# A graph layer's double product in 49 small products instead of 28 large ones, with streams of their own

## The chip, the cores and the metric

The kernel runs on one core of a Trainium2 chip. The metric is the device time of one execution in microseconds (us). The engines that matter here: TensorE (PE, matrix products into the eight banks of PSUM), VectorE (DVE), ScalarE (ACT) and GpSimd (POOL) for elementwise work, and SyncE (SP), which issues all DMA transfers of this kernel from one queue, in order. Each engine works through its own instructions in program order and waits on semaphores of the others.

## The reference

There are 64 graphs of N = 256 nodes with D = 512 features, all in f32. Layer 0 is a three-layer graph convolution with a residual and a layer norm; layer 1 is a graph attention with a residual and a layer norm.

```python
# layer 0
h = relu(adj @ (x @ W1) + b1)
h = relu(adj @ (h @ W2) + b2)
x1 = layernorm(x + adj @ (h @ W3) + b3)
# layer 1
q, k = split(x1 @ Wqk);  v = x1 @ Wv
agg = adj @ (k * mask)
w = mask * sum(q * agg, axis=-1) / sqrt(512)
out = layernorm(x1 + softmax(w, over nodes) * v)
```

The kernel uses M = Wq Wk^T: sum(q * (adj (x1 mask) Wk)) is sum((x1 M) * (adj (x1 mask))). So it needs x1 @ Wv and x1 @ M, the *double product*: x1 times two weights side by side, 512 by 1024 together. Scores come from the M half and the gathered rows gt = adj (x1 mask); values come from the Wv half.

## The kernel before

Graphs go in 32 pairs (G = 2). `front` (line 347) does for pair i: support with W1, aggregate with adj, support W2, aggregate, support W3. `back` (line 376) does for pair i-1: the third product with adj plus residual, layer norm, transposition of x1, the gather gt, and then `attention(0)` and `attention(1)`, the double product of each graph, one after the other. `finish` (line 501) does for pair i-2: softmax, values, second layer norm and output. These three are Python generators; each `yield` ends a step, and `run` (line 537) takes steps in the order of a string with a letter per step: ORDER (line 532) with F, B and E for the 31 steady periods, START for the first pair and END for the last. There is no other scheduler: each engine's instructions stand in the order in which the steps record them.

Every large product uses `seven` (line 102), the seven-product form of a 2x2 block product. With sums of the blocks on both sides, products 1, 7, 6, 2, 5, 3, 4 go into three banks: x collects 1, 6, 5, 3; v collects 7 and 4; y holds 2. In between, ACT copies x to temporaries (t1 after product 1, u after 6, q after 5), and PE's next product into x has to wait for that copy. DVE adds t1, q, u to y and v for the blocks of the result; with `plus`, POOL adds a residual to the temporaries first.

- `support` (line 247): 28 matmuls of 128x256 columns per call. The sums of its left side are POOL's (`a_sums`, line 225: S0 = lower blocks' sum, S1, S2, S3). 
- `aggregate` (line 266): 16 matmuls of 128x256, with relu and bias by ACT.
- `adj_times` (line 301): 14 matmuls of 128x256; its sums are POOL's too (`adj_sums`, `t_sums`).
- `attention(g)` (line 445): for each graph, seven products of two matmuls each of 128x512 columns (two for the halves of the inner dimension). Its weights `mv` are Wv, M and their four differences, kept in SBUF for the whole run; its left side is x1T and four sums of x1T made by POOL.

x1 is transposed by DVE in 32x32 blocks, written to `via` in DRAM and read back by four DMAs (lines 430 to 436), so x1T lies with a stride: elements of one block are 16 elements apart. SP issues per pair: xT of the next pair, via, four x1T reads, out twice, aT, x.

What the steps of the change touch: `seven` (102), `load_w` (140), `make_m` (196), `a_sums` (225), `adj_sums` (286), `t_sums` (296), `front` (347), `back` (376), `finish` (501), the orders (532) and the main loop (548).

Of the kernel before, what the change touches and what calls it, by code (L numbers as in the profile page):

```python
# [20 lines left out]
def gcn_then_graph_attention(ctx: ExitStack, tc: tile.TileContext, xT, xN, adjT, mask, W1, b1, W2, b2, W3, b3,  # L21
                             WqT, WkT, Wv, out):

# [66 lines left out]
    def b_sums(B, Ts, eng):  # L90

        sub = OP.subtract
        eng.tensor_tensor(Ts[2], B[3], B[1], op=sub)  # L93
        eng.tensor_tensor(Ts[0], B[1], B[0], op=sub)
        eng.tensor_tensor(Ts[1], B[3], Ts[0], op=sub)
        eng.tensor_tensor(Ts[3], B[2], Ts[1], op=sub)

    def shaped(shape):
        t = tmp()
        return t.rearrange("p (a b) -> p a b", a=shape[1]) if len(shape) == 3 else t  # L100

    def seven(mm, shape, c11, c12, c21, c22, plus=None):

        x = bank(shape)
        mm(1, x, True)
        t1 = shaped(shape)
        nc.scalar.copy(t1, x)  # L109
        if plus is not None:  # L110
            padd(t1, t1, plus[0])
        yield
        v = bank(shape)
        mm(7, v, True)
        yield
        mm(6, x, False)
        u = shaped(shape)
        nc.scalar.copy(u, x)  # L118
        yield
        y = bank(shape)  # L120
        mm(2, y, True)
        c11(y, t1)
        yield
        mm(5, x, False)
        q = shaped(shape)
        nc.scalar.copy(q, x)  # L126
        if plus is not None:
            padd(q, q, plus[2])
            padd(u, u, plus[1])
        c22(v, q)  # L130
        yield
        mm(3, x, False)
        c12(x)
        yield
        mm(4, v, False)
        c21(v, u)
        yield


    def load_w(w, n):  # L140
# [14 lines left out]
        def end():  # L155
            load(2)
            b_sums(q, ts, nc.vector)
            return {1: q[0], 2: q[2], 3: q[3], 4: ts[3], 5: ts[0], 6: ts[1], 7: ts[2]}
# [11 lines left out]
    warm(10)  # L170
    begin, end = load_w(W1, 1)
    xTs = load_xT(0, begin)
    wl = [end()]
# [6 lines left out]
    for n, w in ((2, W2), (3, W3)):  # L180
        begin, end = load_w(w, n)
        begin()
        wl.append(end())
    aTs[1] = load_adj(1)
    b3b = const.tile([P, D], FP, name="b3b")
    nc.sync.dma_start(b3b, b3.partition_broadcast(P))
    mask_t = const.tile([P, NH, NPAIR * G], FP, name="mask_t")
    nc.sync.dma_start(mask_t, mask.rearrange("p (h b) -> p h b", h=NH))
    mask_s = const.tile([P, NH, NPAIR * G], FP, name="mask_s")
    nc.vector.tensor_scalar(mask_s, mask_t, ISCALE, None, op0=OP.mult)  # L190
# [3 lines left out]
    mv = {}  # L194

    def make_m():

        wq = pool.tile([P, DC, D], FP, name="wqT", tag="r", bufs=1)
        qk = [[wq[:, d] for d in range(DC)],
              [pool.tile([P, D], FP, name="wkT", tag="T", bufs=4) for _ in range(DC)]]  # L200
        for d in range(DC):
            for t, w in ((qk[0][d], WqT), (qk[1][d], WkT)):
                nc.sync.dma_start(t, w[d * P:(d + 1) * P, :])
        m = [pool.tile([P, 2, D], FP, name="m0", tag="v", bufs=2), const.tile([P, 2, D], FP, name="m1")]
        v0 = const.tile([P, 2, D], FP, name="v0")
        nc.sync.dma_start(v0, Wv[:HD].rearrange("(c p) f -> p c f", p=P))
        v1 = const.tile([P, 2, D], FP, name="v1")
        nc.sync.dma_start(v1, Wv[HD:].rearrange("(c p) f -> p c f", p=P))
        yield
        for f in range(DC):  # L210
            pt = bank((P, D))
            for d in range(DC):
                for j in range(DC):
                    nc.tensor.matmul(pt[:, j * P:(j + 1) * P], lhsT=qk[0][d][:, f * P:(f + 1) * P],  # L214
                                     rhs=qk[1][d][:, j * P:(j + 1) * P], start=(d == 0 and j == 0),
                                     stop=(d == DC - 1), skip_group_check=True)
            nc.scalar.copy(m[f // 2][:, f % 2, :], pt)
            yield
        ts = [const.tile([P, 2, D], FP, name=f"mv_{s}") for s in KEYS]
        b_sums((v0, m[0], v1, m[1]), ts, nc.vector)  # L220
        mv.update({1: v0, 2: v1, 3: m[1], 4: ts[3], 5: ts[0], 6: ts[1], 7: ts[2]})
        yield


    def a_sums(blk, eng=nc.gpsimd):
# [3 lines left out]
        S = [pool.tile([P, 2, G, P], FP, name="S", tag="S", bufs=11) for _ in range(4)]  # L229
# [17 lines left out]
    def support(src, w, last=None):  # L247
# [3 lines left out]
        def mm(n, ps, first):  # L251
            for g in range(G):
                for c in range(2):
                    nc.tensor.matmul(ps[:, g], lhsT=src[n][:, c, g], rhs=w[n][:, c], start=(first and g == 0 and c == 0),  # L254
                                     stop=(g == G - 1 and c == 1), skip_group_check=True)
# [10 lines left out]
    def aggregate(C, aT, b):  # L266


        hT = [pool.tile([P, 2, G, N], FP, name="hT", tag="act", bufs=4) for _ in range(2)]
# [16 lines left out]
    def adj_sums(aT):  # L286
# [3 lines left out]
        padd(S[:, 0], blk(1, 0), blk(1, 1))  # L290
        padd(S[:, 1], S[:, 0], blk(0, 0), sub)
        padd(S[:, 2], blk(0, 0), blk(1, 0), sub)
        padd(S[:, 3], blk(0, 1), S[:, 1], sub)
        return {1: blk(0, 0), 2: blk(0, 1), 4: blk(1, 1), 5: S[:, 0], 6: S[:, 1], 7: S[:, 2], 3: S[:, 3]}

    def t_sums(B):
        Ts = [pool.tile([P, G, HD], FP, name="T", tag="T", bufs=4) for _ in range(4)]
# [49 lines left out]
    def front(i, hT, src, aT):  # L347
        C = yield from support(src, wl[0])
        nxt = load_xT(i + 1) if i + 1 < NPAIR else None
        src, last = yield from aggregate(C, aT, bcol[0])  # L350
        C = yield from support(src, wl[1], last)
        src, last = yield from aggregate(C, aT, bcol[1])
        x = load_x(i)
        steps = support(src, wl[2], last)
        next(steps)
        yield
        next(steps)
        yield
        aS = adj_sums(aT)
        next(steps)  # L360
        yield
        for g in range(G):
            next(steps)
            for h in range(NH):
                padd(x[:, g, h, :], x[:, g, h, :], b3b)
            yield
        nS = None
        if nxt is not None:
            nS, first, rest, last = a_sums(lower_first(nxt))
            first()  # L370
            rest()
            last()
        C = yield from steps
        return C, aS, x, nxt, nS

    def back(i, C, aS, x, end):
# [34 lines left out]
        if end:  # L411
# [3 lines left out]
            for h, g in hg:  # L415
                apply(h, g)
            Ts = t_sums(xmb)
            for h, g in hg:
                pt = bank((P, 2, 2, P))
# [3 lines left out]
        else:  # L423
# [3 lines left out]
            for h, g in hg:  # L427
                apply(h, g)
                for k in range(2):
                    nc.vector.transpose(tr[:, :, :, h, k, :, g].rearrange("p q j c -> p c q j"),  # L430
                                        r[:, g, h, k * HD:(k + 1) * HD].rearrange("p (c q j) -> p c q j", c=2, q=4))
            via = dram.tile([4, P, D], FP, name="via")
# [8 lines left out]
        gb = lambda h, j: gt[:, h, :, j * HD:(j + 1) * HD]  # L441
        w = small.tile([P, NH, G], FP, name="w", bufs=2)
        vs = [None] * G

        def attention(g):
            b = i * G + g
            v = pool.tile([P, NH, D], FP, name="v", tag="v", bufs=2)

            def mm(n, ps, first):
                for c in range(2):  # L450
                    nc.tensor.matmul(ps, lhsT=src[n][:, c, g], rhs=mv[n][:, c], start=(first and c == 0),  # L451
                                     stop=(c == 1), skip_group_check=True)

            def score(y, h):
                nc.vector.scalar_tensor_tensor(y, y, mask_s[:, h, b:b + 1], gt[:, h, g, :], op0=OP.mult,
                                               op1=OP.mult, accum_out=w[:, h, g:g + 1])

            def c22(ps, t):
                add(t, ps, t)
                score(t, 1)  # L460
            vs[g] = v
            yield from seven(mm, (P, D), lambda y, t: add(v[:, 0, :], y, t), lambda x: score(x, 0),
                             lambda ps, t: add(v[:, 1, :], ps, t), c22)
        gather = adj_times(aS, xmb, Ts, lambda y, t: add(gb(0, 0), y, t), lambda x: nc.scalar.copy(gb(0, 1), x),
                           lambda v, t: add(gb(1, 0), v, t), lambda v, t: add(gb(1, 1), v, t))
        src, first, rest, last = a_sums(x1b, nc.vector if end else nc.gpsimd)
        if end:
            first()
            rest()
            last()  # L470
            one = attention(0)
            for k in "GMGMGMGMGGGMMM":
                next(gather if k == "G" else one)
                yield
            for _ in gather:
                pass
            for _ in one:
                pass
            tail = finish(i, (r, vs, w), [0])
            for _ in attention(1):  # L480
                next(tail, None)
                yield
            for _ in tail:
                pass
            for _ in finish(i, (r, vs, w), [1]):
                pass
            return
        for _ in range(4):
            next(gather)
            yield  # L490
        first()
        rest()
        last()
        yield from gather
        if i + 2 < NPAIR:
            aTs[i + 2] = load_adj(i + 2)
        for g in range(G):
            yield from attention(g)
        return r, vs, w

    def finish(i, prev, gs=range(G)):

        r, vs, w = prev
# [4 lines left out]
        for k, g in enumerate(gs):  # L508
            for h in range(NH):
                nc.vector.scalar_tensor_tensor(vs[g][:, h, :], vs[g][:, h, :], s[:, h, k:k + 1], r[:, g, h, :],  # L510
# [4 lines left out]
        for k, g in enumerate(gs):  # L515
            for h in range(NH):
                nc.vector.bn_stats(st[:, h, k], vs[g][:, h, :])  # L517
# [6 lines left out]
        for k, g in enumerate(gs):  # L524
            for h in range(NH):
                nc.scalar.activation(vs[g][:, h, :], vs[g][:, h, :], AF.Identity, scale=rs[:, h, k:k + 1],  # L526
# [79 lines left out]
```

## Time and profile before

| | us |
|---|---|
| median of three runs | 2838.85 (2838.0 to 2839.55) |
| the profiled execution | 2837.91 |
| its span, first to last instruction | 2836.1 |
| PE busy | 2810.0 |
| POOL busy | 1437.5 |
| DVE busy | 1120.9 |
| ACT busy | 945.3 |

The span is what the profile covers, and the execution's own time has 1.8 us more around it. A matmul of 128x256 or 128x512 in f32 shows as two records. The records of matmuls overlap, since one begins while the one before drains: the duration of a record (380 ns for 256 columns, 592 for 512) is longer than the distance from start to start. "PE busy" is the union of the records. Lines are those of the kernel before. The mean granted TensorE clock is 0.998.

Groups of the page that the change takes away or changes: L451, the double product, 896 matmuls in all: with x1T as weights 384, with its sums 512; L62 `v<-ps,tmp` and `tmp<-ps,tmp`, the adds from PSUM, 692 ns each; L455, the scores, 881 ns from SBUF and 758 ns from PSUM; L233 to L240 `S<-x1T` on POOL, 2190, 1993, 1524 and 1520 ns, against 1270 for such a sum of tiles that lie dense; L109, L118, L126, ACT's copies of x, about 585 ns each.

### The profile page before, as it was taken

The numbers are of one execution on the slowest core, as the hardware profiler recorded it, in microseconds if no ns is written. First come the engines' busy times: TensorE is split into PE (matmuls) and PEld (weight loads), VectorE is DVE, ScalarE is ACT, GpSimd is POOL, SyncE is SP. The second block draws the span as 40 slices with busy tenths as digits, with TensorE's granted clock in tenths as the row PEclk, the third lists the DMA queues.
The fourth block names the chain that finished last, engine by engine and source line by source line (L and its number), as shares of the span: only waits on it lengthen the run. The fifth ranks groups of instructions, "written<-read, shape, count | busy, mean of one in ns | idle before, by whom it ended". The sixth has DMA issues, their size and how long they took to land.

```text
span 2836.1 us, 29920 instructions
## 1 busy us (share of the span) xinstructions
PE 2810.0 (99%) x11344; PEld 2191.4 (77%) x11344; DVE 1120.9 (40%) x2326; ACT 945.3 (33%) x1517; POOL 1437.5 (51%) x1122
## 2 busy tenths in 40 slices
PE   9999999999999999999999999999999999999997
PEld 8887778877778877787777788777887777877774
DVE  2444334443344443344433444333444334443335
ACT  2333233332333332333323333323333233333333
POOL 4545455445555455554555554556545455445551
PEclk9999999999999999999999999999999999999999
DMA  4211222211222112222122221122221222211210
GB/s 153 67 60 42 65 80 82 82 42 55 67 82 82 54 44 67 82 82 73 44 63 67 82 82 45 53 67 82 82 64 49 67 67 82 82 45 52 67 60 30
DMA packets 63086, 191.00 MB, mean 67 GB/s; under 512 B 5728, under 2 KB 8928, under 8 KB 54880
## 3 DMA queue, kind: packets, MB, share of 16 engines
q1 hardware_dynamic: 62944, 189.10, 21.1%
q8 instruction: 90, 1.47, 0.2%
q14 instruction: 52, 0.43, 0.1%
HBM read 123.02 MB, written 66.06 MB: 67 GB/s over the span
## 4 chain that ended last, share of the span: by engine, by line
PE 97%; DVE 1%; DMA 1%; ACT 1%; issue 0%; SPq 0%; POOL 0%; ACTq 0%; DVEq 0%; POOLq 0%
PE ps L254 41%; PE ps L451 27%; PE ps L275 16%; PE ps L307 13%; PE ps L214 1%; DMA aT<-in_adjT 0%; PE ps L341 0%; PE ps L326 0%; DMA mask_t<-in_mask 0%; ACT v L526 0%; SPq L149 0%; DVE st L517 0%; POOL tmp L65 0%; DMA out<-v 0%; DVE st L388 0%
## 5 line engine op out<-in xcount | busy, mean ns | idle before, releaser
L254 PE MATMUL ps<-w_T,S 128*128 128x256 f32 x2304 | 546.9, 380 | 2.3 <-POOL S L237 1.5
L254 PEld LDWEIGHTS ps<-w_T,S 128*128 128x128 f32 x2304 | 432.5, 190 | 106.6 <-issue 52.1
L275 PE MATMUL ps<-aT,sup 128*128 128x256 f32 x2048 | 472.7, 379 | 0.0
L275 PEld LDWEIGHTS ps<-aT,sup 128*128 128x128 f32 x2048 | 389.1, 190 | 76.1 <-issue 22.2
L62 DVE TENSOR_TENSOR sup<-ps,tmp 128x512 f32<-128x512 f32 x288 | 198.4, 689 | 526.8 <-PE ps L254 338.4
L451 PE MATMUL ps<-mv_T,S 128*128 128x512 f32 x768 | 361.0, 592 | 0.0
L65 POOL TENSOR_TENSOR tmp<-tmp,x 128x512 f32<-128x512 f32 x96 | 120.5, 1270 | 418.8 <-ACT tmp L126 242.3
L278 ACT ACTIVATE hT<-ps,b 128x512 f32<-128x512 f32 x256 | 175.4, 685 | 377.1 <-PE ps L275 377.1
L62 DVE TENSOR_TENSOR v<-ps,tmp 128x512 f32<-128x512 f32 x128 | 88.5, 692 | 535.5 <-PE ps L451 531.8
L118 ACT COPY tmp<-ps 128x512 f32<-128x512 f32 x224 | 131.3, 586 | 486.3 <-PE ps L254 223.4
L109 ACT COPY tmp<-ps 128x512 f32<-128x512 f32 x224 | 130.7, 583 | 418.0 <-PE ps L254 283.7
L126 ACT COPY tmp<-ps 128x512 f32<-128x512 f32 x224 | 130.7, 583 | 339.0 <-PE ps L254 221.4
L254 PE MATMUL ps<-w,hT 128*128 128x256 f32 x1024 | 241.9, 379 | 0.0
L451 PE MATMUL ps<-v,x1T 128*128 128x512 f32 x512 | 240.6, 592 | 0.0
L254 PEld LDWEIGHTS ps<-w,hT 128*128 128x128 f32 x1024 | 194.5, 190 | 46.3 <-issue 14.8
L451 PEld LDWEIGHTS ps<-mv_T,S 128*128 128x128 f32 x768 | 145.8, 190 | 102.1 <-issue 92.3
L233 POOL TENSOR_TENSOR S<-x1T 128x512 f32<-128x512 f32 x31 | 67.9, 2190 | 275.7 <-DMA x1T<-via 275.7
L307 PE MATMUL ps<-T,aS 128*128 128x256 f32 x768 | 200.3, 383 | 0.3 <-ACT tmp L109 0.3
L451 PEld LDWEIGHTS ps<-v,x1T 128*128 128x128 f32 x512 | 146.2, 290 | 69.3 <-issue 17.7
L233 POOL TENSOR_TENSOR S<-hT 128x512 f32<-128x512 f32 x64 | 81.2, 1269 | 220.5 <-ACT hT L278 220.5
L254 PE MATMUL ps<-w,S 128*128 128x256 f32 x768 | 181.5, 379 | 0.7 <-issue 0.7
L93 POOL TENSOR_TENSOR T<-sup 128x512 f32<-128x512 f32 x32 | 41.0, 1281 | 272.8 <-ACT sup L256 272.8
(109 smaller groups left out, 4179.9 us busy)
## 6 DMA issues: line engine op xcount, KB each, us to landing
x<-in_xN SPq DMA_DIRECT2D x32, 1024.0 KB, 5.7
out<-v SPq DMA_DIRECT2D x64, 512.0 KB, 3.3
xT<-in_xT SPq DMA_DIRECT2D x31, 1024.0 KB, 4.9
via<-tr SPq DMA_DIRECT2D x31, 1024.0 KB, 4.3
x1T<-via SPq DMA_DIRECT2D x124, 256.0 KB, 4.7
aT<-in_adjT SPq DMA_DIRECT2D x32, 512.0 KB, 4.3
w<-in_W SPq DMA_DIRECT2D x9, 256.0 KB, 5.2
xT<-in_xT SPq DMA_DIRECT2D x2, 512.0 KB, 5.1
```

The source lines that it names most:

```text
L62: nc.vector.tensor_tensor(o, a, b, op=OP.add)
L65: nc.gpsimd.tensor_tensor(o, a, b, op=op)
L93: eng.tensor_tensor(Ts[2], B[3], B[1], op=sub)
L109: nc.scalar.copy(t1, x)
L118: nc.scalar.copy(u, x)
L126: nc.scalar.copy(q, x)
L233: eng.tensor_tensor(S[2], blk(0, 0), blk(1, 0), op=sub)
L254: nc.tensor.matmul(ps[:, g], lhsT=src[n][:, c, g], rhs=w[n][:, c], start=(first and g == 0 and c == 0), stop=(g == G - 1 and c == 1), skip ...
L275: nc.tensor.matmul(ps[:, g], lhsT=C[k][c // 2][:, g, (c % 2) * P:(c % 2 + 1) * P], rhs=aT[:, k, g], start=(g == 0 and k == 0), stop=(g == ...
L278: nc.scalar.activation(hT[c // 2][:, c % 2], ps, AF.Relu, bias=b[:, c:c + 1])
L307: nc.tensor.matmul(ps[:, g], lhsT=aS[n][:, g], rhs=mov[n][:, g], start=(first and g == 0), stop=(g == G - 1), skip_group_check=True)
L451: nc.tensor.matmul(ps, lhsT=src[n][:, c, g], rhs=mv[n][:, c], start=(first and c == 0), stop=(c == 1), skip_group_check=True)
```

## The change

The double product uses the seven-product form twice. The outer form takes the pair's two graphs together: x1 in 2x2 blocks (rows by inner dimension) times [Wv; M] in blocks (inner dimension by the two weights' halves as before), seven outer products. Each outer product is itself done by seven inner products on 128x128 left blocks and 128x256 right blocks. That makes 49 matmuls of 128x256 per pair in place of 28 of 128x512.

Outer products run in four chains: a = (1, 2), b = (6, 5), c = (7, 4), d = (3). A chain of two puts both outer products in one bank (256 columns each), so that one step has two matmuls and one eviction serves both; d has half of that. Chains a and b alternate step by step, then c and d. The sums on the outer right side are taken so that product 5 has the opposite sign: the outer sum P1 + P6 + P5 is then a difference, and the result blocks are P1+P2, C22 = (P1+P6+P5) + P7, C12 = (P1+P6+P5) + P3 and C21 = C22 + P4 - P5. Chains c and d get the outer sums as the `plus` of `seven`.

- Left side: `attention` copies three blocks of x1T on ACT and makes four sums on DVE (Z), and eight sums on POOL (I) for the inner form.
- Right side: 49 blocks of 128x256 are made once at the start (`make_m`) and stay in DRAM (`w_dram`), not in SBUF. A ring of seven tiles feeds PE: each step's matmuls are followed by the issue of the fetch for seven steps later, 28 fetches per pair on SP's queue (21 of 256 KB and 7 of 128 KB).
- Scores now come from SBUF: `results(g)` after the inner products, once for each graph.
- Streams: the sums on POOL for the next pair (`sums`, letter S), the gather (G) and the double product (M) are generators of their own beside F, B and E; the last pair has two finishing streams X and Y. START, ORDER and END are new strings.
- `seven` with `plus` issues c22 and the addition to u after product 3 instead of after product 5.
- W2 and W3 are loaded and summed inside START (`prepare`), not ahead of it.
- Buffers: hT 4 to 2, S 11 to 8, v two of one graph to one of two graphs; the results R lie in the places of T, x1T and Z.

```diff
@@ seven
         nc.scalar.copy(q, x)
         if plus is not None:
             padd(q, q, plus[2])
+        else:
+            c22(v, q)
+        yield
+        mm(3, x, False)
+        if plus is not None:
+            c22(v, q)
             padd(u, u, plus[1])
-        c22(v, q)
-        yield
-        mm(3, x, False)
         c12(x)
@@ 
+    def prepare():
+        for n, w in ((2, W2), (3, W3)):
+            begin, end = load_w(w, n)
+            begin()
+            yield from end()
...
+        yield from make_m()
+    OUTER = ((1, 2), (6, 5), (7, 4), (3,))
+    INNER = (1, 7, 6, 2, 5, 3, 4)
+    STEPS = "ab" * 7 + "cd" * 7
+    w_dram = [dram.tile([P, 7, len(q), HD], FP, name=f"mv_{k}", bufs=1) for k, q in enumerate(OUTER)]
...
+    RING = 7
+    def fetch(k):
+        if k < NPAIR * len(uses):
+            q, n = uses[k % len(uses)]
+            t = pool.tile([P, 2, HD], FP, name="ring", bufs=RING)
+            nc.sync.dma_start(t[:, :len(OUTER[q])], w_dram[q][:, n])
+            ring[k] = t
@@ make_m
+        for q, outer in enumerate(OUTER):
+            for k, n in enumerate(outer):
+                w = pool.tile([P, 7, HD], FP, name="w7", tag=("Za", "Ia")[place[n] % 2], bufs=1)
+                blk = [B[n][:, c, j * HD:(j + 1) * HD] for c in range(2) for j in range(2)]
+                for i, b in ((1, blk[0]), (2, blk[2]), (3, blk[3])):
+                    nc.scalar.copy(w[:, at[i]], b)
+                yield from b_steps(blk, [w[:, at[i]] for i in (5, 6, 7, 4)], nc.vector)
+                nc.sync.dma_start(w_dram[q][:, :, k], w)
+                yield
@@ back: the old attention(g), a_sums(x1b) and the end's own loop go; the gather becomes a stream
-            def mm(n, ps, first):
-                for c in range(2):
-                    nc.tensor.matmul(ps, lhsT=src[n][:, c, g], rhs=mv[n][:, c], start=(first and c == 0),
-                                     stop=(c == 1), skip_group_check=True)
...
-            yield from seven(mm, (P, D), lambda y, t: add(v[:, 0, :], y, t), lambda x: score(x, 0),
-                             lambda ps, t: add(v[:, 1, :], ps, t), c22)
...
-        for g in range(G):
-            yield from attention(g)
+        put["G"] = gather()
+        put["M"] = attention(i, x1b, w, r, put)
+    def attention(i, x1b, w, r, put):
...
+        for n, b in ((1, x1b(0, 0)), (2, x1b(0, 1)), (4, x1b(1, 1))):
+            nc.scalar.copy(z(n), b)
+        for o, a, b, op in ((z(5), x1b(1, 0), x1b(1, 1), OP.add), (z(6), z(5), z(1), sub), (z(7), z(1), x1b(1, 0), sub),
+                            (z(3), z(2), z(6), sub)):
+            nc.vector.tensor_tensor(o, a, b, op=op)
+        yield
+        for s in range(2):
+            padd(I[s][:, 2], Z[s][:, :, 0], Z[s][:, :, 1], sub)
+            padd(I[s][:, 0], Z[s][:, :, 1], Z[s][:, :, 3])
+            padd(I[s][:, 1], I[s][:, 0], Z[s][:, :, 0], sub)
+            padd(I[s][:, 3], Z[s][:, :, 2], I[s][:, 1], sub)
+            yield
...
+            def mm(n, ps, first):
+                wt = ring.pop(at[0])
+                for k, o in enumerate(outer):
+                    nc.tensor.matmul(ps[:, k], lhsT=left[n](place[o]), rhs=wt[:, k], start=(first and k == 0),
+                                     stop=(k == len(outer) - 1), skip_group_check=True)
+                fetch(at[0] + RING)
+                at[0] += 1
...
+        for n, k in enumerate(STEPS):
+            if n == 14:
+                add(B[:, 0], B[:, 0], A[:, 0])
+                yield
+                nc.vector.tensor_tensor(B[:, 0], B[:, 0], B[:, 1], op=sub)
+                yield
+                add(v[:, :, 0], flat(A[:, 0]), flat(A[:, 1]))
+                yield
+                C = pool.tile([P, 2, G, 2, HD], FP, name="R", tag="Za", bufs=1)
+                run.update(c=inner(2, C, B), d=inner(3, B[:, :1], B[:, :1]))
+            if n == 26:
+                yield from results(0)
+            next(run[k])
+            yield
+        yield from results(1)
@@ orders
-    ORDER = ("F E F" + " B F" + " B F E" * 2 + " B B E F E F" + " B F E" + " B F B F F B B F F" +
-             " B F B F B F E B B E F F" + " B F E B F E" + " B F E B F E B B F B F B F B" + " B F B F B B F B F B F B")
+    ORDER = ("BFFFEFFEBEFBBBFBFBBFBFEFBFBFBEBBBGFEGSFFEGGFEGEEFEMFMFFFGMMGSMEMMMMMMMMMMMSMMMMMMFSM"
+             "FMMFSMMMMFFSMMMSEMMSMFMFSMSMSMM")
```

## The prediction

> **What bounds the kernel now.** I read the page's busy line and its 40 slices first, then the chain that ended last, then the waits of PE alone, then PE in order of time inside one period.
>
> ```profile
> span 2836.1 us, 29920 instructions
> ...
> PE 2810.0 (99%) x11344; PEld 2191.4 (77%) x11344; DVE 1120.9 (40%) x2326; ACT 945.3 (33%) x1517; POOL 1437.5 (51%) x1122
> ...
> q1 hardware_dynamic: 62944, 189.10, 21.1%
> ...
> PE 97%; DVE 1%; DMA 1%; ACT 1%; issue 0%; SPq 0%; POOL 0%; ACTq 0%; DVEq 0%; POOLq 0%
> ```
>
> PE is busy for the whole span and is 97% of the chain; the other engines and DMA are half idle. Overlapped records can hide a PE that is not at its peak, so I check its pace:
>
> ```profile
> 910.80 1.88 PE L451 MATMUL ps<-mv_T,S 128*128 128x512 f32 x4
> 912.52 1.88 PE L451 MATMUL ps<-v,x1T 128*128 128x512 f32 x4
> 914.23 1.03 PE L254 MATMUL ps<-w,hT 128*128 128x256 f32 x4
> ...
> 1050.88 5.34 PE L275 MATMUL ps<-aT,sup 128*128 128x256 f32 x24
> 1056.06 1.89 PE L254 MATMUL ps<-w,hT 128*128 128x256 f32 x8
> ```
>
> From start to start, 8 records of 512 columns take 914.23-910.80 = 3.43 us, 0.429 each; 24 records of 256 columns take 5.18 us, 0.216 each. An f32 matmul is two records, so 0.858 and 0.432 us. SP's issues of the next xT mark the period, 86.9 us:
>
> ```profile
> 960.75 0.33 SPq L72 DMA_DIRECT2D xT<-in_xT  x1
> ...
> 1047.66 0.33 SPq L72 DMA_DIRECT2D xT<-in_xT  x1
> ```
>
> Its matmuls: 84 (three supports) + 32 (two aggregates) + 28 (two adjacency products) = 144 of 256 columns, 62.2 us; 28 of 512, 24.0 us; small transposes of the softmax 0.7. Sum 86.9: PE has no hole in a steady period. What is taken from PE's work comes off one for one, as long as nothing else becomes late.
>
> **1. PE work.** 28 matmuls of 512 columns (24.02 us) become 49 of 256 (49 x 0.432 = 21.15): -2.87 us per pair. Weight loads go from 56 to 98 records per pair, but a 190 ns load lies under a 216 ns matmul already in the rows of L254 and L275, and the 290 ns loads of the strided x1T go. 31 of the 32 double products lie in steady periods: **-89.0 us**. The last is in part 5.
>
> **2. The other engines, per period of 84 us.** DVE has 35.0 now (1120.9/32). It loses 10 operations of the old scores and adds (7.9) and gains 14 adds from PSUM at 0.69 or less (8.5), 4 sums into Z, 3 combinations of 1024, 4 scores, 2 adds. The last 13 have both operands in SBUF. Rows for such operations: 0.69 alone, 1.31 and 1.76 beside POOL (lines 233, 236 at the end); for 1024 elements 1.22 and 2.17. So DVE comes to 47 to 55 us. ACT: 29.5, less 6 copies of 0.585, plus 17, three of them from strided x1T: 35 to 37. POOL: 44.9, less the four strided sums (7.2), plus eight I sums (1.27 or about 1.0) and six additions (1.27 or 0.73): 53. All under 84, so none becomes the bound by its total.
>
> The Trainium skill, SBUF — State Buffer, § Who interferes with whom, speaks against this change: VectorE with two SBUF inputs and a GpSimd instruction that reads SBUF exclude each other for the whole instruction. The rows above agree in direction; by the rule 13 DVE operations could each wait one whole POOL sum of 1.27 us, an estimate of 16 us more on DVE, 64 to 72 of 84, and the sum below stays.
>
> **3. Who waits for whom on the way.** I followed the order of the built program from one support 1 to the next, with PE at 0.432 per matmul and the rows' durations for the rest.
> - *x1T to Z.* The trace has 11.3 us from the issue of via to the first sum on x1T. via can be issued 16.3 us after xT, as now, so Z starts 44 us into the period. ACT's three copies end at 46 to 47.5 (0.585 to 1.17 each; strided ACT reads have no row, POOL's strided sum takes 1.7 times the plain one), and the first inner product is due at 48.8. The hT evictions queue behind these copies on ACT, due about 4 us later. Cover 1.3 to 2.8 us; costs nothing.
> - *I sums.* The first is due on PE at 51.4 and ends at 47.5 (49 at worst); the third at 53.1 against 50 to 51.5.
> - *One copy between two accumulations.* Products 5 and 3 of one chain have a single 0.864 us step between them. This line shows what it needs:
>
> ```profile
> 17.30 0.59 ACT L126 COPY tmp<-ps 128x512 f32<-128x512 f32 x1 [2.87 <-PE ps L254]
> ```
>
>   PE's slot before it ended at 15.37 + 8 x 0.216 = 17.10 and PE went on at 17.98: 0.88 us. Loss 0.02 per pair, nothing.
> - *Softmax.* Its two transposes now stand 3.68 us apart (6.9 before). The end of the trace shows the chain: 3.31 us from 2810.74 to 2814.05, table load included. Cover 0.4.
> - *The residual product of B*: c22 and the addition to u now stand behind product 3. c22 has to be done before product 4 writes the same bank, with 1.73 us of F between; the statistics then end at 22.3 and hT_2, which waits behind them on ACT, at 23.3, asked at 25.1. Nothing.
> - *Shared buffers* (v single, hT two, S eight, R in the places of T, x1T and Z): the closest are v, written at 65 when its last out has landed at 57, and T, written at 81 when R's last reader ends at 69.5 (combinations at 2.17). Nothing.
> - *POOL's b3b additions, adjacency sums, S and T sums* end at least 2 us before PE or DVE asks; behind the wait for x stands S_3, asked 6 us later.
>
> **4. The ring of weights.** 28 fetches per pair are new on SP (21 of 256 KB, 7 of 128 KB), each issued when a step's matmul ends, at 0.33 to 0.47 us of SP. SP is in order: aT and the second out<-v stand between them, and that out waits for ACT's last activation, done 9 us before. Seven tiles are there at the start; then step k+7 needs a fetch that was issued 6.05 us before. A lone 256 KB read lands in 3.0 to 3.3 us (the first of the four x1T reads). In sixteen steps of 0.864 the queue must also carry aT and out, four units of 256 KB. With the first fetch on the wire at 52.3, the tenth tile arrives at 52.3 + 7 units + 0.1, due at 57.5. What is a unit?
>
> ```profile
> 0.00:23.00 23.00, 17.66 (x79) 14.66 (x80) 11.77 (x17) 3.63 (x5) 6.42 (x10) 1.00 0.96 327
> ```
>
> In the loading stretch (clock 1.00, then DMA share 0.96, 327 GB/s) full engines would move 341 GB/s: 0.77 us, a tile 0.3 us late. By the page's whole-run share (189.1 MB in 21.1% of 2836.1: 316 GB/s) 0.83 us, 0.75 late. A single slice of the window 900:987 reached 383 GB/s: 0.68, not late. I take the saturated stretch, the nearest: 0.3 us in each of 31 periods, **+9** (0 to +23).
>
> The Trainium skill, DMA: Bandwidth & Descriptors, § Bandwidth, advises batches of 1 MiB or more, and its § Anatomy of one DMA — SWDGE (gpsimd) path (another queue than SP's) gives 2.0 us plus bytes over 436 GB/s, an estimate of 2.6 us for 256 KB. One fetch at a time, that would stop every step; seven deep, it is shorter than 6.05 and costs 0. The measured 3.0 to 3.3 leads.
>
> **5. Start and end.** *Start:* DVE no longer holds support 1's evictions behind the sums of W2 and W3 (PE waits 0.72 and 0.77 at 17.98 and 20.71); one of these goes, about 1.7 us with what follows. The M product moves forward to where its last weights land (issued 19.38, 5.5 us): no gain, up to 4 lost. **-1.5** (-3 to +4). *End:* after the last F matmul (2765.1) the trace runs 71.0 us, two old products (3.4) among them. After: E's four bn_stats (0.68) and three activations (0.8) stand ahead of B's chain on DVE and ACT, so the last double product starts 28.7 us after F instead of 23.1; it is 3 us shorter; but PE stops for about 4.3 us ahead of its last two steps until DVE has the scores of g=0, and behind the last step there are two more adds, two scores and an add, about 5 us. I get 76 us. With the two steps that no longer lie behind F (-3.4+0.4) the end costs 76-71+3 = **+8** (+3 to +13).
>
> **Sum.** -89 + 9 - 1.5 + 8 = -73.5. The profiled execution took 2837.9 (span 2836.1), 0.9 below the median of 2838.85: 2764.4 against it, 2765 for a median. Ends: 2838.85-89+0-3+3 = 2750 and 2838.85-89+23+4+13 = 2790.
>
> **The rivals.**
> - *Slower: the ring's DMA sets the pace.* If a 256 KB unit takes s, the fourteenth tile arrives at 52.3 + 11s + 0.1, due at 60.9: 11s - 8.5 late per pair. The 81 us of parts 1 and 5 are gone at 2.6 us per pair, s = 1.01. For it: 2 KB packets in a 14 KB stride are not in this trace, and the seven-deep ring has only 0.4 us of cover at s = 0.70. Against it: every saturated stretch shows 0.68 to 0.83. At s = 1.2 the time is 2838.85-81+31 x 4.7 = 2904.
> - *DVE and POOL block each other longer than summed up.* Then Z, I and the scores come late in each period: two sums at 1.76 instead of 0.69 eat the cover, and 0.8 to 1.6 us per pair are lost: 2783 to 2807. For it: the rows of 1.76 and 2.17. Against it: POOL is idle while Z is made.
> - *The change doesn't bring what it counts*, since PE waits on several small things (copies behind L617, x late): 1.5 to 2.6 us per pair, 2805 to 2838. Against it: covers of 1 to 6 us.
> - *No stall at all and a cheap end:* 2750 or a little under.
>
> **How the numbers follow.** Forecast with its range 2750 to 2790: 0.62. A cleaner run, under 2750: 0.04. DVE and POOL, up to 2807: 0.11. Several small waits: 0.07, of which 0.02 within 0.2% of 2838.85 (about what a measurement of this kernel can tell from no change). Ring slower than break-even: 0.16, nearly all slower. Range 2748 to 2815 holds about 0.77 and leaves the slower rival out. Faster 0.82, same 0.02, slower 0.16.
>
> **What the profile after would show.** Period between xT loads 84.0 to 84.6 (part 1 and 4); PE's waits: <-DMA ring under 0.5 us per pair if part 4 holds, above 2.6 if the slower rival does; waits <-ACT Z, <-POOL I or <-DVE w in steady periods near 0 (part 3), else the second rival; POOL busy about 1700 us, DVE 1500 to 1760, ACT 1130 to 1180 (part 2); behind the last F matmul 76 us with a PE hole of some 4 us before the last two ring steps (part 5). I would be wrong most if 2 KB reads at a 14 KB stride are slow, or if x1T lands over 2 us later than now.

## The result and the profile after

The changed kernel takes 2833.94 us (median of four runs, 2828.76 to 2836.84), beside 2838.47 for the kernel before on the same chip: a ratio of 0.9981 with a 95% interval of 0.9964 to 0.9999. That is 0.19% faster, less than the 0.2% that the prediction took for no change, and 69 us above the 2765 that was forecast. The profiled execution took 2833.77. (Of the four executions of e5 below, the profiled one ran at a third of TensorE's pace, 8150 us; e5's time is that of the other three, and the trace of that kernel is e9's.)

The page after, busy time, ring queue and the chain that ended last:

```profile
span 2832.0 us, 36770 instructions
...
PE 2740.0 (97%) x12688; PEld 2371.6 (84%) x12688; DVE 1703.6 (60%) x2898; ACT 1151.9 (41%) x1888; POOL 1786.5 (63%) x1446
...
q1 hardware_dynamic: 197568, 401.10, 44.5%
...
PE 86%; DMA 7%; ACT 3%; DVE 3%; issue 1%; POOL 0%; SPq 0%; ACTq 0%; DVEq 0%; POOLq 0%
PE ps L306 37%; PE ps L543 18%; PE ps L328 15%; PE ps L364 14%; DMA ring<-mv 6%; DVE e L391 1%; ACT L388 1%; ACT e L388 1%; ACT tmp L126 1%; ACT tmp L117 1%; PE ps L248 1%; PE ps L398 0%; DVE gt L560 0%; DMA xT<-in_xT 0%; DVE w L97 0%
```

PE fell from 97% of the chain to 86%. What came in its place has names: ring<-mv, the fetches of the double product's weights, and the softmax's e on DVE and ACT. The waits of PE alone, as us in total, number of times, longest, say the same:

```profile
PE ps L543 <- DMA ring<-mv: 33.8, 39, 2.3
PE ps L398 <- DVE e L391: 22.6, 28, 3.6
PE ps L383 <- DVE gt L560: 9.4, 3, 4.0
PE ps L476 <- DVE r L460: 2.9, 2, 1.7
PE ps L306 <- DVE sup L65: 2.1, 1, 2.1
PE ps L306 <- POOL S L289: 1.8, 2, 1.5
```

The two upper rows recur in nearly every pair; the others belong to the start and the end. Before, no wait recurred; the longest row there was this one:

```profile
PE ps L341 <- DVE e L334: 3.7, 2, 2.5
```

This view misses part of a wait that stands inside a group. Counted from start to start of PE's records, at the first record of each step and beyond 0.216 us, the ring loses 45.3 us over 32 pairs: 35.2 at the tenth tile of a pair (in 29 of the pairs, 1.21 us each), 10.1 at the ninth (in 27 pairs, 0.37 each), nothing at the other 26 tiles.

Between SP's issues of xT, averaged over the last 29 periods, a period takes 86.34 us, against 86.90 before and 84.0 in the forecast. So 2.3 us of the 2.87 that the matmuls saved per pair are lost again to waits: about 1.4 to the ring, 0.7 to the softmax, the rest to pieces of 0.08 to 0.1 us.

How one pair loses at the ring: PE and then SP, in order of time (start, duration, line, what; in brackets the idle time and its end).

```profile
1339.35 3.62 PE L543 MATMUL ps<-ring,I 128*128 128x256 f32 x16
1342.80 1.89 PE L543 MATMUL ps<-ring,Z 128*128 128x256 f32 x8
1344.80 1.10 PE L543 MATMUL ps<-ring,I 128*128 128x256 f32 x4
1346.81 2.91 PE L543 MATMUL ps<-ring,I 128*128 128x256 f32 x12 [0.91 <-DMA ring<-mv]
```

```profile
1337.81 0.34 SPq L230 DMA_DIRECT2D ring<-mv  x1
1338.71 0.33 SPq L84 DMA_DIRECT2D aT<-in_adjT  x1
1339.54 0.32 SPq L230 DMA_DIRECT2D ring<-mv  x1
1339.95 0.38 SPq L620 DMA_DIRECT2D out<-v  x1
1340.43 4.61 SPq L230 DMA_DIRECT2D ring<-mv  x6
```

The issues are on time, one fetch whenever PE frees a tile. Between the eighth tile's fetch (1337.81) and the tenth's (1340.43) stand aT and the second out, 512 KB each. In the trace the eighth tile landed at 1340.51, aT at 1344.00, the ninth at 1344.66, out at 1346.33, the tenth at 1346.67; PE goes on at 1346.81. From then on tiles land 0.68 us apart and PE never waits for them. What the 16 DMA engines did meanwhile, in 40 slices of 0.75 us from 1335 on (busy share in tenths, then GB/s):

```profile
DMA  0000089986799999999885968689998585048789
GB/s 0 0 0 0 0 139 330 284 216 123 254 393 399 404 402 388 407 355 243 287 264 182 310 128 303 164 212 412 426 415 358 169 280 176 0 71 306 183 276 341
```

From 1338.75 to 1343.25 they are busy for 60% of the time or more and yet move only 123 to 330 GB/s, 224 in the mean; then, 90% busy or more, 388 to 407.

How the softmax loses, from its first transposes (L383) to its second (L398); `T<-sup,T` are GpSimd's sums for B's product, and `tmp<-tmp,x` adds the residual x to the first copy of that product:

```profile
1378.47 0.38 PE L383 MATMUL ps<-ident,w 128*2 128x128 f32 x2
1378.48 2.94 POOL L97 TENSOR_TENSOR T<-sup,T 128x512 f32<-128x512 f32 x2
1378.89 0.41 DVE L385 TENSOR_REDUCE nmax<-ps 2x1 f32<-2x256 f32 x1
1379.28 1.28 ACT L388 ACT_TABLE_LOAD   x1
1380.58 0.47 ACT L388 ACTIVATE e<-ps,nmax 2x256 f32<-2x256 f32 x1
1381.16 0.15 DVE L390 RECIPROCAL rtot<-tot 2x1 f32<-2x1 f32 x1 [1.86 <-ACT e L388]
1381.35 1.43 DVE L391 TENSOR_SCALAR e<-e,rtot 2x256 f32<-2x256 f32 x1
1381.37 1.27 POOL L68 TENSOR_TENSOR tmp<-tmp,x 128x512 f32<-128x512 f32 x1
1382.93 0.25 PE L398 MATMUL ps<-ident,e 2*128 2x2 f32 x2 [0.62 <-DVE e L391]
```

The scaling of e, 2x256 elements, took 0.341 us in every period before (least, median and greatest duration in ns, then first and last start). Here it takes 1.43 in most, starts with POOL's tmp+x and ends 0.14 us behind it. First the kernel before, then the changed one:

```profile
L334 DVE TENSOR_SCALAR e<-e,rtot x33: 340/341/342, 166.0 to 2826.4; 2x256 f32<-2x256 f32 x31, 1x256 f32<-1x256 f32 x2
L391 DVE TENSOR_SCALAR e<-e,rtot x33: 341/1435/1461, 171.8 to 2821.2; 2x256 f32<-2x256 f32 x31, 1x256 f32<-1x256 f32 x2
```

### The profile page after: what moved, and what is told of

The parts are those of the page before. It is cut to its first block, busy times and chain, and to the rows that moved or that the text cites. A ratio compares the mean times of both kernels' runs of the same rounds, so it can differ in the third digit from the quotient of the medians.

```text
span 2832.0 us, 36770 instructions
## 1 busy us (share of the span) xinstructions
PE 2740.0 (97%) x12688; PEld 2371.6 (84%) x12688; DVE 1703.6 (60%) x2898; ACT 1151.9 (41%) x1888; POOL 1786.5 (63%) x1446
## 4 chain that ended last, share of the span: by engine, by line
PE 86%; DMA 7%; ACT 3%; DVE 3%; issue 1%; POOL 0%; SPq 0%; ACTq 0%; DVEq 0%; POOLq 0%
PE ps L306 37%; PE ps L543 18%; PE ps L328 15%; PE ps L364 14%; DMA ring<-mv 6%; DVE e L391 1%; ACT L388 1%; ACT e L388 1%; ACT tmp L126 1%; ACT tmp L117 1%; PE ps L248 1%; PE ps L398 0%; DVE gt L560 0%; DMA xT<-in_xT 0%; DVE w L97 0%
## 5 line engine op out<-in xcount | busy, mean ns | idle before, releaser
L65 DVE TENSOR_TENSOR R<-ps,tmp 128x512 f32<-128x512 f32 (+1 forms) x384 | 235.4, 620 | 455.1 <-PE ps L543 350.2
L543 PE MATMUL ps<-ring,I 128*128 128x256 f32 x1792 | 435.3, 383 | 36.5 <-DMA ring<-mv 33.8
L328 PE MATMUL ps<-aT,sup 128*128 128x256 f32 x2048 | 457.7, 379 | 0.0
L543 PEld LDWEIGHTS ps<-ring,I 128*128 128x128 f32 x1792 | 332.8, 190 | 107.0 <-ACT tmp L134 40.3
L134 ACT COPY tmp<-ps 128x512 f32<-128x512 f32 (+1 forms) x288 | 158.3, 561 | 473.6 <-PE ps L306 251.3
L68 POOL TENSOR_TENSOR I<-Z 128x384 f32<-128x384 f32 (+1 forms) x128 | 173.3, 1374 | 262.6 <-ACT Z L521 244.9
L543 PE MATMUL ps<-ring,Z 128*128 128x256 f32 x1344 | 327.7, 380 | 0.0
L68 POOL TENSOR_TENSOR tmp<-tmp,R 128x512 f32<-128x512 f32 x192 | 214.9, 1140 | 169.8 <-DVE R L580 141.5
L126 ACT COPY tmp<-ps 128x512 f32<-128x512 f32 (+1 forms) x288 | 158.1, 560 | 358.9 <-PE ps L543 173.8
L117 ACT COPY tmp<-ps 128x512 f32<-128x512 f32 (+1 forms) x288 | 158.7, 563 | 326.7 <-PE ps L364 120.2
L543 PEld LDWEIGHTS ps<-ring,Z 128*128 128x128 f32 x1344 | 256.4, 191 | 34.7
L68 POOL TENSOR_TENSOR x<-x,b3b 128x512 f32<-128x512 f32 x128 | 176.8, 1382 | 73.2 <-DMA x<-in_xN 63.8
```

The costliest lines, as they stand in the source:

```text
L65: nc.vector.tensor_tensor(o, a, b, op=OP.add)
L68: nc.gpsimd.tensor_tensor(o, a, b, op=op)
L328: nc.tensor.matmul(ps[:, g], lhsT=C[k][c // 2][:, g, (c % 2) * P:(c % 2 + 1) * P], rhs=aT[:, k, g], start=(g == 0 and k == 0), stop=(g == ...
L543: nc.tensor.matmul(ps[:, k], lhsT=left[n](place[o]), rhs=wt[:, k], start=(first and k == 0), stop=(k == len(outer) - 1), skip_group_check= ...
```

## The experiments

**Theory.** The miss is two waits that come back in each pair. (1) The tenth tile is late because aT and the second out take the DMA engines' time ahead of it. (2) VectorE's scaling of e is held for the length of a GpSimd operation. **Rivals.** For the ring: fetches with 2 KB rows at a 14 KB stride are slow in themselves; or only the order within one queue counts. For the softmax: its chain is too long for 3.5 us of matmuls whoever scales, or VectorE is slow beside any other traffic.

Each run was compared with the kernel before. All times and trace figures follow together:

| run | time, us | ratio to before [95%] | period, us | PE waits: ring / e |
|---|---|---|---|---|
| the change | 2833.94 | 0.9981 [0.9964, 0.9999] | 86.34 | 33.8 / 22.6 |
| e1, scale on ACT | 2812.73 | 0.9906 [0.9891, 0.9921] | 85.50 | 27.6 / 6.4 |
| e2, aT late | 2799.14 | 0.9859 [0.9845, 0.9874] | 85.28 | 8.6 / 23.4 |
| e3, out early | 2784.15 | 0.9809 [0.9795, 0.9824] | 84.62 | 0.6 / 19.2 |
| e4, all three | 2769.31 | 0.9755 [0.9738, 0.9771] | 84.13 | none / 6.4 |
| e5, no tmp+x | 2812.11 | 0.9906 [0.9889, 0.9923] | | |
| e6, out on ACT's queue | 2839.57 | 1.0001 [0.9990, 1.0012] | 86.23 | 36.8 / 21.5 |
| e7, e4 and end | 2769.62 | 0.9755 [0.9740, 0.9769] | | none / 3.9 |
| e8, layout | 2823.86 | 0.9951 [0.9935, 0.9968] | 85.92 | 25.5 / 21.3 |
| e9, e5 again | 2812.77 | 0.9908 [0.9888, 0.9928] | 85.52 | 29.3 / 6.4 |

And when tiles land, medians over 29 pairs in us behind the issue of the eighth tile's fetch, as the trace's issue and landing times give them:

| run | aT landed | ninth | second out landed | tenth | eleventh |
|---|---|---|---|---|---|
| the change | 6.18 | 6.86 | 8.44 | 9.00 | 9.66 |
| e2, aT late | (28.0) | 4.80 | 6.83 | 7.62 | 8.73 |
| e3, out early | 5.27 | 5.96 | (-4.12) | 6.66 | 7.34 |
| e4, all three | (27.3) | 4.48 | (-4.06) | 5.66 | 6.43 |
| e6, out on ACT's queue | 6.30 | 7.95 | 8.49 | 8.93 | 9.60 |
| e8, layout | 6.02 | 6.64 | 8.03 | 8.67 | 9.39 |

In e4, where no tile is late, PE starts the ninth step at 6.71 and the tenth at 7.58 in the median; where it has to wait, it starts 0.13 behind the landing. So the ninth tile is in time when it lands by 6.58, and the tenth by 7.45.

### e1: the scaling of e on ScalarE

```diff
-        nc.vector.tensor_scalar(e, e, rtot, None, op0=OP.mult)
+        nc.scalar.activation(e, e, AF.Identity, scale=rtot)
```

> The softmax's scaling of e (2x256) goes from VectorE to ScalarE; nothing else moves. Theory (VectorE's scaling is held up by GpSimd's sum tmp+x that starts beside it: 1.43 us instead of the 0.34 us of the kernel before): the scaling is done about 0.9 us earlier, TensorE's wait at the transposes of e (20 to 23 us in all) falls under 5 us, and the time falls from 2834 by 18 to 23 us, to 2811-2816. Rival (the softmax chain is too long for the 3.5 us of matmuls between its transposes, whoever scales): the wait stays at 15 us or more and the time at 2826-2836. TensorE's wait for the ring stays at 45 us (40 to 50) by both.

Measured: 2812.73, inside the theory's range. The scaling itself became longer than an undisturbed one on VectorE, and yet the recurring wait is gone (durations as above; of the waits, total, times, longest):

```profile
L391 ACT ACTIVATE e<-e,rtot x33: 507/507/508, 173.6 to 2799.0; 2x256 f32<-2x256 f32 x31, 1x256 f32<-1x256 f32 x2
```

```profile
PE ps L543 <- DMA ring<-mv: 27.6, 38, 1.8
PE ps L383 <- DVE gt L560: 9.3, 3, 3.9
PE ps L398 <- ACT e L391: 6.4, 2, 3.7
```

The 6.4 us that stay are two waits at the end of the program, where the chain has no cover. So the chain is not too long in itself. The gain of 21 us is 16 of this wait and 6 of the ring's, whose wait was expected to stay where it was; the ring's order of fetches is the same, its tenth tile landed 0.07 us earlier in the median, and why it lost less is open (e9, with the same fetches, lost less too, 29.3).

### e5 and e9: the GpSimd sum left out

```diff
-        if plus is not None:
+        if plus is not None and plus[0] is not None:
             padd(t1, t1, plus[0])
...
-                             plus=(xb(0, 0), xb(1, 0), xb(1, 1)))
+                             plus=(None, xb(1, 0), xb(1, 1)))
```

Here the scaling stays on VectorE and only POOL's tmp+x beside it goes; one block of r lacks x.

> The first of the three residual sums of B's product, GpSimd's tmp+x that starts beside VectorE's scaling of e, is left out (so x is missing from one block of r); the scaling stays on VectorE and nothing is moved. Theory (it is this GpSimd operation that holds VectorE's scaling for its whole length): the scaling takes 0.34 to 0.45 us in nearly every period, TensorE's wait at the transposes of e falls from 20-23 us to 4-8, the time from 2834 to 2808-2818. Rival 1 (the scaling is slow beside any work of another engine, ScalarE's or the DMA's): it stays at 1.4 us, 2828-2836. Rival 2 (GpSimd's next operation simply takes the place of the one left out): the scaling takes 0.8 us or more, the wait stays above 12 us. The ring's wait stays at 28-45 us by all.

> The same kernel as the run that leaves out the first residual sum of B's product, to get a trace at the usual pace of TensorE (x is missing from one block of r). Theory (GpSimd's sum tmp+x holds VectorE's scaling of e): the scaling takes 0.34 us in nearly all of 33 cases, TensorE's waits at the transposes of e come to 4-8 us instead of 22.6, the time to 2810-2816. Rival: the scaling takes 0.8 us or more and the wait stays above 12 us.

Measured: 2811.94 to 2814.06 in e5 and 2812.77 in e9, the same gain as by moving the scaling. The trace of e9:

```profile
L391 DVE TENSOR_SCALAR e<-e,rtot x33: 340/341/1024, 173.6 to 2798.5; 2x256 f32<-2x256 f32 x31, 1x256 f32<-1x256 f32 x2
```

```profile
1369.41 2.94 POOL L97 TENSOR_TENSOR T<-sup,T 128x512 f32<-128x512 f32 x2
1370.21 1.28 ACT L388 ACT_TABLE_LOAD   x1
1371.51 0.47 ACT L388 ACTIVATE e<-ps,nmax 2x256 f32<-2x256 f32 x1
1372.10 0.15 DVE L390 RECIPROCAL rtot<-tot 2x1 f32<-2x1 f32 x1 [1.86 <-ACT e L388]
1372.28 0.34 DVE L391 TENSOR_SCALAR e<-e,rtot 2x256 f32<-2x256 f32 x1
```

The T sums end as the scaling starts, no POOL operation follows them, and the scaling is back at 0.34 us with everything else as it was. Together with e1 this settles the second wait: the GpSimd operation is the cause, not ScalarE's, PE's or the DMA's traffic.

The Trainium skill, SBUF — State Buffer, § Who interferes with whom, lists tensor_scalar among the VectorE operations that can take the port pair shared with GpSimd, and says that the later of two then waits for the whole instruction. The durations here, 0.34 alone and 1.43 beside 1.27 of POOL, agree. Which of the two came later can't be read from the recorded starts: the scaling's is 0.02 us ahead of tmp+x, but GpSimd's T sum is still running then.

### e2, e3 and e4: what stands ahead of the tenth tile

e2 moves the load of aT out of `gather` to behind the last c/d fetch; e3 moves one step of `finish` in the order; e4 is e1, e2 and e3 together.

```diff
 # e2
-                    if i + 2 < NPAIR:
-                        aTs[i + 2] = load_adj(i + 2)
...
+            if n == 21 and i + 2 < NPAIR:
+                aTs[i + 2] = load_adj(i + 2)
             if n == 26:
                 yield from results(0)
 # e3: the twelfth E, which issues the second out
-    ORDER = ("...GEEFEMFMFFFGMMGSMEMMMMMM..."
+    ORDER = ("...GEEFEMFEMFFFGMMGSMMMMMMM..."
```

> The load of aT for the pair after next is issued 22 us later, behind the last fetch of the c/d tiles instead of ahead of the ninth tile's fetch. Theory (512 KB of aT stand in the queue ahead of the tenth tile, two units of 0.68 us): the tenth tile comes 1.4 us earlier, TensorE's wait for the ring falls from 45 us to 0-10, the time to 2790-2800. Rival 1 (the second out, issued between the ninth and the tenth fetch, is what delays it): the wait stays at 30 us or more, 2818-2834. Rival 2 (fetches of 2 KB packets are too slow for the steps of 0.86 us whatever stands ahead): wait unchanged at 40-50, 2830-2836. Rival 3 (the load only delays something else at its new place): a new wait of 20 us or more at the last ring steps or in the next period's aggregation.

> The second out of finish is issued about 4.3 us earlier, in front of the eighth tile's fetch instead of between the ninth and the tenth; aT stays where the change put it. Theory (it is bytes ahead of the tenth tile that matter, aT's and out's alike): the tenth tile comes up to 1.4 us earlier, but the ninth does not, so TensorE's wait for the ring falls from 45 us to 8-25 and the time to 2797-2815. Rival 1 (aT alone delays the fetches, since a load behind the outs is slow to land: 5.3 us): the wait stays at 35 us or more, 2824-2834. Rival 2 (2 KB fetches too slow in themselves): unchanged, 2830-2836.

> The three edits together: scaling of e on ScalarE, aT behind the last c/d fetch, second out ahead of the eighth tile. Theory: ring wait under 5 us, wait at the transposes of e under 5 us, period 84.2-84.6 us instead of 86.34, time 2834 - 45 - 21 = 2768 (2760-2780), which is below both kernels. Rival (when these waits go, another one comes last, such as VectorE or GpSimd sums that are busy 60% of the span): period 85.0 us or more, 2790-2815.

Measured: e2 2799.14, as the theory had it; e3 2784.15, better than its range of 2797 to 2815: its tenth tile came 2.34 us earlier where at most 1.4 was expected, and the ninth, which was not expected to move, 0.90 earlier; e4 2769.31, in its range and 2.45% under the kernel before (its waits at e are 6.4 us, not under 5, all at the end of the program). In e3 PE runs through the place where it stopped:

```profile
1318.67 1.89 PE L543 MATMUL ps<-ring,Z 128*128 128x256 f32 x8
1320.40 3.71 PE L543 MATMUL ps<-ring,I 128*128 128x256 f32 x16
1323.95 3.19 PE L543 MATMUL ps<-ring,Z 128*128 128x256 f32 x14
```

The landing table explains the sizes. With neither transfer ahead (e4) the tenth tile lands at 5.66, that is 3.07 us behind its own issue at 2.59. aT alone puts 1.00 us on top (e3), out alone 1.96 (e2), both 3.34. Against 7.45 the tile has a cover (the time by which it is early) of 1.8 us in e4 and 0.8 in e3; it is 0.2 late in e2 and 1.55 late in the change. The last is what a pair of the change loses at the two tiles together: the ninth, due at 6.58 and landed at 6.86, takes part of it, and the tenth the rest. With a tenth tile 0.2 late in the median, e2 loses in 16 of 32 pairs: 13.0 us by the count from start to start, 8.6 by the waits. Neither transfer alone makes the ring late by much; the two together do. (In e3 the out is issued 9.4 us earlier in the trace, not 4.3.)

e4's page shows a kernel bound by PE again:

```profile
PE 97%; DVE 1%; POOL 0%; issue 0%; ACT 0%; DMA 0%; SPq 0%; ACTq 0%; DVEq 0%; POOLq 0%
```

```profile
1273.84 0.33 SPq L75 DMA_DIRECT2D xT<-in_xT  x1
...
1357.96 0.33 SPq L75 DMA_DIRECT2D xT<-in_xT  x1
...
1442.08 0.33 SPq L75 DMA_DIRECT2D xT<-in_xT  x1
```

Its periods of 84.12 us are, within 0.1, those that part 1 of the prediction counted for the change itself. No third wait of any size took the place of the two. This version beats both kernels.

### e6 and e8: which property of the transfers

```diff
 # e6
-            nc.sync.dma_start(out[i, ...
+            nc.scalar.dma_start(out[i, ...
 # e8 (and the write of w_dram at the start alike)
-    w_dram = [dram.tile([P, 7, len(q), HD], ...
+    w_dram = [dram.tile([7, P, len(q), HD], ...
...
-            nc.sync.dma_start(t[:, :len(OUTER[q])], w_dram[q][:, n])
+            nc.sync.dma_start(t[:, :len(OUTER[q])], w_dram[q][n])
```

> Both outs are issued on ScalarE's queue instead of SyncE's, at the same place of the order; aT stays ahead of the ninth tile. Theory (the 16 DMA engines' time is what is short: the second out's 512 KB take 2 us of it wherever they are queued): the out still shares the engines with the ninth and tenth tile, the tenth lands 8 to 9 us after the eighth's issue (9.0 before), TensorE's wait for the ring falls at most by half, to 15-40 us, time 2802-2832. Rival (it is only the order within one queue: a fetch behind an out waits until the out is through): with the out in another queue the tenth tile lands 6.5 to 7 us after the eighth's issue, the wait is under 8 us, 2786-2796.

> The changed kernel with one difference: in DRAM each of the 28 tiles of the ring is one contiguous block of 256 or 128 KB, so that the 2 KB rows of a fetch follow each other instead of standing 14 KB apart (aT, out and the scaling of e are as the change has them). Theory (what is late is queue time and latency behind aT and out, not the stride): the tenth tile still lands 8.7 to 9.2 us after the eighth's issue, TensorE's wait for the ring stays at 38-50 us, time 2826-2838. Rival (reading 2 KB at a stride of 14 KB is what makes the fetches slow): the tenth lands at 7.5 us or less, the wait under 12 us, 2788-2803.

Measured, e6: 2839.57, above the theory's 2802 to 2832, with a wait of 36.8 us (15 to 40 expected) and the tenth tile at 8.93 (8 to 9). The wait did not fall at all. Another queue does not help: the tenth tile lands as late as before, and the ninth, beside which out now runs (it is issued at 1.74 instead of 2.14), even 1.09 us later. What delays the tenth tile is not its place behind out in SP's queue. That leaves the time of the DMA engines.

e8: 2823.86, against 2826 to 2838 expected; the tenth tile lands 0.33 us earlier, at 8.67 (8.7 to 9.2 expected), and the wait is 25.5, or 35 by the count from start to start in place of 45.3 (38 to 50 expected). The time missed the theory's range by 2 us, and the rival's by 21. Not all of the 10 us need be the stride's: in e1 and e9, whose fetches are those of the change, the tenth tile landed at 8.93 and 8.80 and the ring lost 39 us by the same count, and the intervals of e8 and the change touch. So the stride is at most a small part of the cause, a quarter of what the place of aT or out does.

### e7: the end

```diff
-    END = ("BEEBEEBEEBBBBEBBBBEB...
+    END = ("BBEBEBEEBEEBBEBBBBEB...
```

> On top of the three edits of before (2769 us), the order at the end is changed alone: the last two double steps of the softmax's transposes stand behind two and three products of B instead of behind one (B B E B E instead of B E E B B). Theory (the holes of 4.0 and 2.6 us after the last matmul of F are filled by B's next two products of 1.73 us): the two waits fall from 6.6 to 2-4 us and the time by 2 to 4.5 us, to 2765-2767. Rival (VectorE's and GpSimd's chain behind it, not TensorE, sets the end: what is not waited for here is waited for at the transposes of r): within 1 us of 2769.

Measured: 2769.62 beside 2769.31, the rival's outcome by the time. The waits changed names, and became a little less:

```profile
PE ps L383 <- DVE gt L558: 5.4, 2, 3.7
PE ps L364 <- POOL T L97: 4.1, 2, 3.3
PE ps L398 <- ACT e L391: 3.9, 1, 3.9
```

In e4 they were 9.4 for gt and 6.4 for e (the lines stand two lower there than in the change). B's next product now stands first in PE's queue and waits for POOL's T instead. The equal times do not settle the rivals, though: from the last matmul of F to the end the trace of e7 takes 79.06 us and that of e4 80.12, but e7's third load of xT, at a place that the edit doesn't touch, is issued 2.46 us later (98.41 against 95.94). By the traces this order takes about 1 us off the end, less than the 2 to 4.5 expected, and a start of another length hides it. Why the start differs from trace to trace (95.9 to 98.4 us) is open.

## Why the prediction was wrong

- **Part 1, PE's work: right.** -2.87 us per pair. e4 shows nearly all of it once the waits are gone: 86.90 to 84.13 is 2.77.
- **Part 2, totals: right for two of three.** DVE 1703.6 (1500 to 1760 said) and ACT 1151.9 (1130 to 1180); POOL 1786.5 where 1700 was said, nearly all of the difference in operations that took longer than the rows used for them: two I sums of 128x512 per pair 1.75 us for 1.27, the three additions tmp+R of that shape 1.55 for 1.27, the two T sums that read only sup 1.70 beside 1.28 and 1.30 before. VectorE's 1703.6 are 53.2 per pair, in the 47 to 55 counted, and not the 64 to 72 that the prediction put beside them. None became the bound by its total, as said.
- **Part 3, "Softmax ... Cover 0.4": wrong, -0.7.** The step took the chain from the end of the trace of before, where POOL does nothing, and set its 3.31 us against 3.68. In the steady period POOL works through the T sums and tmp+x just there, and the scaling takes 1.43 instead of 0.34: chain 3.31 + 1.09 = 4.40, lost 0.7 per period, some 20 us. The interference was on the same page of the prediction, but as 16 us on VectorE's total, where it does not matter. The place to look for it was each chain with a cover under 1.3 us, one POOL operation.
- **Part 4, "the tenth tile arrives at 52.3 + 7 units + 0.1": right tile, wrong size, 1.4 in place of 0.3 per pair.** The moment of use was right: 57.5 is 8.7 us behind the first ring step (48.8), and in e4 the tenth step starts 8.63 behind it (the eighth tile's fetch is issued 1.05 behind the first step's start, and 7.58 follow). The arrival was not. The formula's 57.8 is 9.0 behind the first step; the tile landed at 1.05 + 9.00 = 10.05, and PE went on 0.13 later still. What was mis-sized is the unit. From the landing of the eighth tile (2.67) to that of the tenth (9.00) six units of 256 KB, two of aT, the ninth tile, two of out and the tenth tile, took 6.33 us: 1.06 each, where 0.77 was taken from the loading stretch and 0.83 stood there as a bound. That is 1.7 us too much; the eighth tile, 0.65 us ahead of the formula, took part of it back. The rows of the DMA engines show the same: 224 GB/s in the mean where 341 was taken, and the saturated pace of 0.68 us per tile only behind the tenth. Why the engines move so little there, though they are mostly busy, no run shows. Ring in all: 45 us where 9 (at most 23) stood.
- **Part 5, start: wrong, +4.3 where -1.5 stood.** The third xT load is issued at 96.06 us instead of 91.75. Of the two waits of before, the one at 20.71 did go, but the one of 0.72 stayed and new ones came: 0.77 twice behind ACT's copy of tmp and 2.07 for VectorE's sup. These are read from the trace alone; no run took them apart, and in other traces the same load is issued as late as 98.41. **End: the place right, the size 3 short.** From the last F matmul to the end it takes 78.87 us, 76 said; the hole before the last two ring steps is 3.68, 4.3 said. e7's order of the waits at its beginning took about 1 us off.
- **The sum.** Against the profiled execution the forecast was 2764.4 and 2833.8 came, 69.4 more: ring 36, softmax 20, start 6, end 3, and about 4 in pieces of 0.08 to 0.1 us.
- **The rivals.** "The ring's DMA sets the pace" was not it: it needed 1.01 us per 256 KB up to the fourteenth tile. Up to the tenth it was 1.06, but behind it the tiles land 0.68 apart, and all but the ninth and tenth of a pair are on time. "DVE and POOL block each other" was the right mechanism at another place than the one named (Z, I, scores). The price that came true, 1.5 to 2.6 us per pair, was that of "PE waits on several small things", with a chance of 0.07, though by two causes with a name rather than many.

## What to carry to other kernels

In this ring the critical tile landed 3.07 us behind its own issue, plus 1.0 to 2.3 us for each 512 KB transfer issued among the fetches, more than the pace of a loading stretch gave. So add up everything that is issued there, compare with the moment of use, and place other transfers where the ring has slack. Here, issuing a 512 KB write 9 us earlier (1.8% of the time) did more than a different queue (nothing) or a contiguous layout (at most 0.4%). And where the cover of a chain is less than one GpSimd operation, put its small VectorE step on ScalarE or look up in the trace what GpSimd does just then: a duration from a stretch where GpSimd is idle does not hold.

## What was not expected of the hardware

- A VectorE operation on 2x256 elements took 1.43 us instead of 0.34 beside a GpSimd sum, and ended 0.14 us behind it, though the trace has it starting 0.02 us earlier. GpSimd's T sum was just ending (1378.48 + 2.94 = 1381.42), and the next GpSimd operation was through before the scaling; without that next operation the scaling, started in the same way, took 0.34.
- A 512 KB write to DRAM put more on the tenth tile than a 512 KB read: 1.96 against 1.00 us (2.34 against 1.38 when both are there). The read is issued 1.24 us earlier, though, and ahead of the ninth tile too; no run puts the two at the same place, so that it is the write as such is not shown.
- The aT read lands 5.3 us after its issue between the ring's fetches (4.3 in the kernel before); e4's second out, issued away from the ring, lands 3.2 us after its issue.
